# Three targets in turn for the last accumulated blocks of a mixture-of-experts stage

## The chip, the cores and the metric

The kernel runs on one core of a Trainium2 chip. The metric is the device time of one execution in microseconds (us). Four runs of the kernel before the change are given with their median; one more execution was recorded by the hardware profiler, and its trace gives all durations used here.

## The reference

The input `x` has 8 batches of 512 tokens with 256 numbers each, so 4096 tokens. Four layers follow each other, each of the form `x = x + layer(layernorm(x))`: a linear recurrence with projections, a mixture of experts, causal attention with 16 heads, and the same mixture of experts once more. Only the mixture matters for the change:

```python
topk_idx, tw = _route(x, router_w, bias)        # 4 of 16 experts for each token
combine = (one_hot(topk_idx, E) * tw[..., None]).sum(1)
h = einsum('td,edf->etf', x, gate_w);  u = einsum('td,edf->etf', x, up_w)
y = einsum('etf,efd->etd', silu(h) * u, down_w)
routed = einsum('etd,te->td', y, combine)       # sum of a token's 4 experts
sh = silu(x @ sh_gate_w) * (x @ sh_up_w) @ sh_down_w
return routed + sh                              # the layer adds x to this
```

So each of the 4096 output rows of the last layer is a sum of six terms: the row that went in, the shared experts' row, and four experts' rows with their weights.

## The kernel before

The kernel has four stages, one for each layer. In the two mixture stages (function `routed`, called with `i = 0` and, last, `i = 1`) the token rows have been sorted by expert into a DRAM tensor, and blocks of 128 rows of one expert are worked on one after the other. `LIKELY` = 136 blocks are run by `run(0, LIKELY)`; a rarely needed second run for blocks 136 to 142 stands in a branch before it. The blocks are ordered by batch: `DONE[b]` says from which block on no row of batch `b` can occur. The values are 31, 47, 63, 79, 95, 111, 127 for batches 0 to 6, then 135 for the first half of batch 7, and 143 for its second half.

For a block `n`, SP (SyncE) loads its rows (L982 to L990), ACT and DVE copy the two weight matrices (L1006), TensorE multiplies by them (L1033), ACT and DVE form the activation (L1041, L1043), and, two blocks later, `down(n)` multiplies by the third matrix (L1063), ACT scales the result by the routing weight (L1072), and POOL (GpSimd) issues an indirect DMA that adds the 128 result rows to rows of a DRAM tensor (L1073, destination `part`, source `rows`). In what follows this DMA is "the accumulation of block `n`".

Two accumulations on the same rows must not overlap. Therefore there are two DRAM tensors for each mixture, `parts[i][0]` and `parts[i][1]`, one with the stage's input in it and one with the shared experts' result, and blocks go to them in turn (`n % 2`). An accumulation waits until the one two blocks before it has landed; this wait stands in POOL's queue in front of the DMA, so that everything behind it on POOL waits too:

```python
if len(accs) > 1:
    behind_of(acc, accs[-2])
```

At the end the two parts are summed. For batches 0 to 6 of the last stage this is done in the middle of the run: some blocks after `DONE[b]`, `begin(b)` issues two loads of 512 KB on SP (L1609) that wait for the last two accumulations which can concern the batch (function `apart`), and later `add_up` adds them on DVE (L1613) and stores the sum in the output (L1614). The last batch is done in two halves of 256 rows behind block 135:

```python
plan.setdefault(LIKELY, []).append(begin_last)      # loads of the first half
routed(1, table, plan)
load_both(first + half, half, ends[1], (nc.sync, nc.scalar))
for n in range(2):
    add_up(first + n * half, half, ends[n])
```

`begin_last` declares the loads of the first half free of block 135's accumulation, and behind those of blocks 133 and 134. The loads of the second half wait for the last accumulation on the tensor that they read. The part 0 load of the second half is on SP's queue, the part 1 load on ACT's.

Small DMAs that prepare memory, among them the zeros for the spare rows of the parts (L351), are in a list `later`, of which each batch of the first stage issues a share behind its load of the next input (`Scan.load`, on SP's queue).

Of the kernel before, what the change touches and what calls it, by code (L numbers as in the profile page):

```python
# [10 lines left out]
FP = mybir.dt.float32  # L11
# [4 lines left out]
P = 128  # L16
SQ = 32
QUAD = P // SQ
B, T, D = 8, 512, 256
NT = T // P  # L20
# [14 lines left out]
NTOK = B * T  # L35
BLK = P
# [6 lines left out]
LIKELY = TK * NTOK // BLK + E // 2  # L43
# [9 lines left out]
DONE = [TK * rows // BLK + E - 1 for rows in KEYS]  # L53
# [29 lines left out]
def tile_hybrid_block(  # L83
# [22 lines left out]
    nc = tc.nc  # L106
# [8 lines left out]
    def bank(shape, name: str, kind: str = "one"):  # L115
        kind = instead.get(kind, kind)
        return stage[kind].tile(shape, FP, tag=kind, name=name)

    def banks_of(**many):
        pools = ExitStack()  # L120
        for kind, bufs in many.items():
            stage[kind] = pools.enter_context(
                tc.tile_pool(name=f"ps_{kind}", bufs=bufs, space=bass.MemoryType.PSUM)
            )
        return pools

    dram = ctx.enter_context(tc.tile_pool(name="dram", bufs=1, space=bass.MemoryType.DRAM))
# [2 lines left out]
    xg = [dram.tile([NROW, ROW], FP, name=f"xg_{i}") for i in range(2)]  # L130


    parts = [[dram.tile([NTOK + BLK, D], FP, name=f"part_{i}_{j}") for j in range(2)] for i in range(2)]

    x_tiles = {}

    def values(name: str):
        return work.tile([P, NT * (H * VC + 32 - VC)], FP, tag="v", name=name)
# [93 lines left out]
    def load_expert(e: int):  # L232
        at = e * WEXP
        gu = w_all[:, at : at + 2 * KD * F].rearrange("p (s k f) -> p s k f", k=KD, s=2)
        nc.sync.dma_start(out=gu[:, 0], in_=gate_w[e].rearrange("(p k) f -> p k f", p=P))
        nc.sync.dma_start(out=gu[:, 1], in_=up_w[e].rearrange("(p k) f -> p k f", p=P))
        nc.sync.dma_start(
            out=w_all[:, at + 2 * KD * F : at + WEXP].rearrange("p (k d) -> p k d", k=KF),
            in_=down_w[e].rearrange("(k p) d -> p k d", p=P),
        )  # L240
# [95 lines left out]
    zeros = const.tile([P, ROW], FP, name="zeros")  # L336
# [8 lines left out]
    later = [lambda e=e: load_expert(e) for e in range(E - OUT)]  # L345
    for i in range(2):
        later.append(
            lambda i=i: free(f"xg{i}", nc.sync.dma_start(out=xg[i][E * REG :, :], in_=zeros))
        )
        for j in range(2):  # L350
            later.append(lambda i=i, j=j: nc.sync.dma_start(out=parts[i][j][NTOK:, :], in_=zeros[:, 0:D]))  # L351
    shares = B - 2


# [144 lines left out]
    def kb4(name: str):  # L499
        return work.tile([P, NT, D], FP, tag="kb4", name=name, bufs=KB)  # L500
# [109 lines left out]
    every = [small.tile([P, len(KEYS), E], FP, tag="every", name=f"every_{i}", bufs=1) for i in range(2)]  # L610
# [196 lines left out]
    accs = []  # L807

    def apart(load, done: int):


        for n, acc in enumerate(accs):
            if n >= done:
                tc.declare_no_dep(load.ins, acc.ins, reason="no row of these tokens in later blocks")
            elif n >= done - 2:
                behind_of(load, acc)
        tc.add_to_no_dep_group("sums", load.ins)

    def behind_of(made, other):
        tc.add_manual_dep(  # L820
            made.ins,
            other.ins.name,
            mybir.DependencyInfo(mybir.DependencyClass.Sync, mybir.DependencyReason.DATA),
            reason="accumulations on the same rows",
        )

    def free(group: str, made):

        tc.declare_no_dep(made.ins, group=group, reason="rows of their own")
        tc.add_to_no_dep_group(group, made.ins)  # L830
# [103 lines left out]
    def routed(i: int, table, beside):  # L934

        weight_at, row_at, expert, many = table
# [122 lines left out]
        def down(n: int):  # L1059
            w, _, rows, act, gain = held.pop(n)  # L1060
            py = bank([P, D], f"pyr_{i}_{n}", "y")
            for f in range(KF):
                nc.tensor.matmul(  # L1063
                    py,
                    lhsT=act[:, f * P : (f + 1) * P],
                    rhs=w_all[:, bass.ds(w + 2 * KD * F + f * D, D)],
                    start=(f == 0),
                    stop=(f == KF - 1),
                )

            y = rows[:, ROW : ROW + D]
            nc.scalar.mul(y, py, gain[:, TK : TK + 1])  # L1072
            acc = nc.gpsimd.indirect_dma_start(  # L1073
                out=parts[i][n % 2],
                out_offset=bass.IndirectOffsetOnAxis(
                    ap=rows[:, D + 2 * TK : D + 2 * TK + 1].bitcast(U32), axis=0
                ),
                in_=y,
                in_offset=None,
                compute_op=ALU.add,  # L1080
            )
            if len(accs) > 1:
                behind_of(acc, accs[-2])
            tc.declare_no_dep(acc.ins, group="sums", reason="no row of those tokens in later blocks")
            accs.append(acc)

        def run(first: int, last: int):
# [18 lines left out]
            for n in range(first, last + 2):  # L1106
                load_to(n + AHEAD)
                if n + 2 < last and n + 2 not in known:
                    values(n + 2)
                if n + 1 < last:  # L1110
                    fetch(n + 1)
                if n + 2 not in heads and n + 2 < last:
                    turn(n + 2)
                if n < last:
                    up(n)
                if n + 1 in heads and n + 1 < last:
                    turn(n + 1)
                if n - 2 >= first:
                    down(n - 2)
                    for work_beside in beside.get(n - 1, ()):  # L1120
                        work_beside()
# [3 lines left out]
            many, min_val=0, max_val=NBLK, skip_runtime_bounds_check_because="a count of blocks"  # L1125
# [74 lines left out]
    class Attention:  # L1200
# [6 lines left out]
        bursts, parts = {}, {}  # L1207
# [167 lines left out]
    def prepared(b: int):  # L1375
# [17 lines left out]
        def begin():  # L1393
            held["added"] = load_sum(0, b, free_home("v", f"more_{b}"), lambda load: apart(load, first))
# [16 lines left out]


        plan = [begin, add, lambda: step(NT), lambda: step(1), lambda: step(NT + 1)]
        after = {}
        for at, do in zip((4, 12, 13, 14, 15), plan):
# [186 lines left out]
    with banks_of(big0=2, big1=2, misc=2, y=2):  # L1602

        def rows_at(of, first: int, many: int):
            return of[first : first + many, :].rearrange("(p t) d -> p t d", p=P)

        def load_both(first: int, many: int, both, queues=(nc.sync, nc.sync)):
            return [
                queue.dma_start(out=both[j], in_=rows_at(parts[1][j], first, many)) for j, queue in enumerate(queues)  # L1609
            ]  # L1610

        def add_up(first: int, many: int, both):
            tc.keep_in_program_order(nc.vector.tensor_add(both[0], both[0], both[1]))  # L1613
            nc.sync.dma_start(out=rows_at(out.rearrange("b t d -> (b t) d"), first, many), in_=both[0])  # L1614

        def homes(b: int):
            other = values(f"sum_{b}_1")[:, 0 : NT * D].rearrange("p (t d) -> p t d", t=NT)
            return xpool.tile([P, NT, D], FP, tag="x", name=f"sum_{b}_0"), other

        sums, plan = {}, {}  # L1620

        def begin(b: int):
            sums[b] = homes(b)
            for load in load_both(b * T, T, sums[b]):
                apart(load, DONE[b])

        for b in range(B - 1):
            wait, stay = (4, 12) if b < B - 2 else (1, 5)
            plan.setdefault(DONE[b] + wait, []).append(lambda b=b: begin(b))
            plan.setdefault(DONE[b] + stay, []).append(lambda b=b: add_up(b * T, T, sums[b]))  # L1630


        first, half, ends = (B - 1) * T, T // 2, []

        def begin_last():
            both = homes(B - 1)
            ends.extend([tile[:, n * NT // 2 : (n + 1) * NT // 2, :] for tile in both] for n in range(2))
            for load in load_both(first, half, ends[0]):
                apart(load, DONE[B - 1])

        plan.setdefault(LIKELY, []).append(begin_last)
        routed(1, table, plan)
        load_both(first + half, half, ends[1], (nc.sync, nc.scalar))
        for n in range(2):
            add_up(first + n * half, half, ends[n])

# [41 lines left out]
```

## Time and profile before

| what | value |
|---|---|
| runs | 1638.76, 1637.65, 1644.29, 1636.44 us |
| median of the four runs | 1638.21 us |
| profiled execution, own time | 1639.39 us |
| profiled execution, span of its instructions | 1637.7 us |
| mean granted TensorE clock | 0.985 |
| SP issues, loads of sums (L1609) | 17 on SP, 1 on ACT |
| SP issues, zeros of the parts (L351) | 4, 327 to 507 ns each, at 22.0 to 146.2 us |
| accumulations (L1073) | 272, 1542 to 2293 ns on POOL, median 1550 |
| additions of sums (L1613) | 7 of 128x1024 (about 1.21 us), 2 of 128x512 (0.69 us) |

The profile gives times in microseconds from the first instruction. PE is TensorE, PEld its weight loads, DVE VectorE, ACT ScalarE, POOL GpSimd, and SP SyncE; `SPq` and `ACTq` are DMA issues on these engines' queues. A row of the timeline has start, duration, engine, line, operation, tiles, and in brackets how long the engine was idle before and what seems to have ended that. The last stage's 136 blocks begin at about 1241 us. The releaser in brackets is inferred, and a wait for several things is put down to the one that came last.

### The profile page before, as it was taken

The numbers are of one execution on the slowest core, as the hardware profiler recorded it, in microseconds if no ns is written. First come the engines' busy times: TensorE is split into PE (matmuls) and PEld (weight loads), VectorE is DVE, ScalarE is ACT, GpSimd is POOL, SyncE is SP. The second block draws the span as 40 slices with busy tenths as digits, with TensorE's granted clock in tenths as the row PEclk, the third lists the DMA queues.
The fourth block names the chain that finished last, engine by engine and source line by source line (L and its number), as shares of the span: only waits on it lengthen the run. The fifth ranks groups of instructions, "written<-read, shape, count | busy, mean of one in ns | idle before, by whom it ended". The sixth has DMA issues, their size and how long they took to land. (4 is left out here: it accounts for less than half of the span.)

```text
span 1637.7 us, 34092 instructions
## 1 busy us (share of the span) xinstructions
PE 1580.4 (97%) x10030; PEld 1161.2 (71%) x10030; DVE 1004.5 (61%) x3264; ACT 779.5 (48%) x1622; POOL 775.0 (47%) x639
## 2 busy tenths in 40 slices
PE   8899998999999999999899999999999999999995
PEld 6466665679999999983444454444558999999995
DVE  6877764434466444437898889887834445444552
ACT  3343442235555555546544544454214555555553
POOL 4366754635556555540013432433432555555554
PEclk9999998999999999999999999999999999999998
DMA  5454423547777776641323433343745767777776
GB/s 169 137 178 154 149 99 125 180 92 109 117 122 108 107 98 96 93 68 46 80 83 114 121 109 108 106 118 98 261 138 90 109 112 127 119 138 131 136 136 128
DMA packets 282766, 196.88 MB, mean 120 GB/s; under 512 B 168689, under 2 KB 262673, under 8 KB 282577
## 3 DMA queue, kind: packets, MB, share of 16 engines
q1 hardware_dynamic: 230016, 121.50, 29.2%
q0 software_dynamic: 51984, 72.09, 24.8%
q8 instruction: 85, 1.39, 0.4%
q10 hardware_dynamic: 576, 1.05, 0.2%
q14 instruction: 105, 0.85, 0.2%
HBM read 91.29 MB, written 103.23 MB: 119 GB/s over the span
## 5 line engine op out<-in xcount | busy, mean ns | idle before, releaser
L1073 POOL DMA_INDIRECT part<-rows x272 | 426.8, 1569 | 342.9 <-ACT rows L1072 224.0
L798 POOL DMA_INDIRECT xg<-sorted_m,slots_m x256 | 270.4, 1056 | 260.6 <-ACT slots_m L795 128.8
L1033 PEld LDWEIGHTS ph<-rows,gate 128*128 128x128 f32 x2160 | 277.5, 191 | 32.7 <-ACT rows L1016 21.6
L1033 PE MATMUL ph<-rows,gate 128*128 128x128 f32 x2160 | 291.7, 278 | 0.5 <-ACT rows L1016 0.5
L1033 PE MATMUL ph<-rows,up 128*128 128x128 f32 x2160 | 285.3, 275 | 0.0
L1063 PE MATMUL pyr<-w_all,rows 128*128 x1088 | 279.5, 380 | 1.4 <-DVE rows L1043 1.4
L1033 PEld LDWEIGHTS ph<-rows,up 128*128 128x128 f32 x2160 | 262.9, 192 | 0.0
L1006 DVE COPY up<-w_all 128x512 f32 x270 | 120.0, 445 | 226.1 <-PE ph L1033 205.3
L1006 ACT COPY gate<-w_all 128x512 f32 x270 | 166.4, 617 | 124.3 <-DVE up L1006 60.1
L1043 DVE TENSOR_TENSOR rows<-ph,rows 128x256 f32<-128x256 f32 x272 | 115.5, 425 | 155.0 <-ACT rows L1041 75.3
L1295 ACT ACTIVATE w_all<-ps_a 128x1024 f32<-128x1024 f32 x160 | 155.2, 1021 | 105.4 <-PE ps_a L1285 93.3
L1063 PEld LDWEIGHTS pyr<-w_all,rows 128*128 128x128 f32 x1088 | 186.8, 192 | 15.8 <-DVE rows L1043 1.6
L1072 ACT ACTIVATE rows<-pyr,gain 128x256 f32<-128x256 f32 x272 | 128.7, 473 | 78.5 <-PE pyr L1063 58.0
L1041 ACT ACTIVATE rows<-ph 128x256 f32<-128x256 f32 x272 | 104.3, 384 | 117.2 <-PE ph L1033 101.1
L1174 PE MATMUL pd_m<-sd_sb,act_m 128*128 128x256 f32 x512 | 120.2, 383 | 6.2 <-DVE act_m L1162 3.4
L1285 PE MATMUL ps_a<-w_all 32*128 32x384 f32 (+3 forms) x1024 | 107.4, 474 | 10.9 <-ACT w_all L1295 9.7
L1174 PEld LDWEIGHTS pd_m<-sd_sb,act_m 128*128 128x128 f32 x512 | 95.9, 190 | 31.1 <-issue 9.4
L1305 DVE SCALAR_TENSOR_TENSOR w_all<-w_all,causal 128x512 f32<-128x512 f32 (+1 forms) x160 | 91.8, 574 | 28.2 <-ACT w_all L1295 26.2
L1285 PEld LDWEIGHTS ps_a<-w_all 32*128 32x128 f32 x1024 | 46.2, 187 | 68.6 <-ACT w_all L1295 36.0
L1146 PE MATMUL pg_m<-w_all,su_sb 128*128 128x512 f32 x192 | 93.2, 609 | 0.0
L1146 PE MATMUL pg_m<-w_all,sg_sb 128*128 128x512 f32 x192 | 92.8, 605 | 0.0
L1321 PE MATMUL po_a<-w_all,v_a 128*32 128x512 f32 (+3 forms) x1024 | 92.0, 450 | 0.0
(222 smaller groups left out, 1924.1 us busy)
## 6 DMA issues: line engine op xcount, KB each, us to landing
rows<-xg SPq DMA_DIRECT2D x720, 32.0 KB
rows<-xg SPq DMA_DIRECT2D x92, 134.0 KB
part<-x SPq DMA_DIRECT2D x16, 512.0 KB
w_all<-in_L_ffn_gate_w_dram SPq DMA_DIRECT2D x29, 256.0 KB
w_all<-in_L_ffn_up_w_dram SPq DMA_DIRECT2D x29, 256.0 KB
w_all<-in_L_ffn_down_w_dram SPq DMA_DIRECT2D x29, 256.0 KB
part<-ys_m SPq DMA_DIRECT2D x14, 512.0 KB
sum<-part SPq DMA_DIRECT2D x14, 512.0 KB
```

The costliest lines, as they stand in the source:

```text
L798: nc.gpsimd.indirect_dma_start(out=xg[i], out_offset=bass.IndirectOffsetOnAxis(ap=slots[:, at : at + 1], axis=0), in_=rows[:, t, :], in_of ...
L1006: copy(here, w_all[:, bass.ds(held[n][0] + half * KD * F, KD * F)])
L1033: nc.tensor.matmul(ph[s][:, f * P : (f + 1) * P], lhsT=both[s][:, k * F + f * P : k * F + (f + 1) * P], rhs=rows[:, ROW + k * P : ROW + (k ...
L1041: nc.scalar.activation(act, ph[0], AF.Silu)
L1043: made = nc.vector.tensor_mul(act, ph[1], act)
L1063: nc.tensor.matmul(py, lhsT=act[:, f * P : (f + 1) * P], rhs=w_all[:, bass.ds(w + 2 * KD * F + f * D, D)], start=(f == 0), stop=(f == KF - 1),
L1072: nc.scalar.mul(y, py, gain[:, TK : TK + 1])
L1073: acc = nc.gpsimd.indirect_dma_start(out=parts[i][n % 2], out_offset=bass.IndirectOffsetOnAxis(ap=rows[:, D + 2 * TK : D + 2 * TK + 1].bit ...
L1146: made = nc.tensor.matmul(dst, lhsT=w[:, k, f * P : (f + 1) * P], rhs=xnT[:, k, :], start=(k == 0), stop=(k == KD - 1),)
L1174: nc.tensor.matmul(py[:, j, :], lhsT=acts[n][:, f, t * P : (t + 1) * P], rhs=shared[n][3][:, f, :], start=(n == 0 and f == 0), stop=(n == ...
L1285: nc.tensor.matmul(ps[j // 2][:, j % 2, col : col + n], lhsT=k_sb[w][r, o, c * P : (c + 1) * P], rhs=q_sb[r, o, c * P : T], start=True, st ...
L1295: nc.scalar.activation(es[two], ps[two], AF.Exp, scale=ATT_SCALE)
```

## The change

A third DRAM tensor is made for the last mixture, `parts[1][2]`. Its rows 3584 to 4223 (the last batch and the spare rows) are filled with zeros by five DMAs of 128 KB in the list `later`. For blocks 128 to 135 of the last stage the target is `n % 3` instead of `n % 2`, and the accumulation waits for the one three blocks before it. The last batch's sum is made of three parts, with a third load for each half and one more addition for each half. The loads of all sums are issued in reversed order of their parts, and they wait for one more accumulation (three instead of two before `DONE`).

```diff
-    parts = [[... for j in range(2)] for i in range(2)]
+    parts = [[... for j in range(2 + i)] for i in range(2)]
...
+    for at in range(NTOK - T, NTOK + 1, P):
+        later.append(lambda at=at: nc.sync.dma_start(out=parts[1][2][at : at + P, :], in_=zeros[:, 0:D]))
...
-            elif n >= done - 2:
+            elif n >= done - 3:
                 behind_of(load, acc)
...
+            many = 3 if i == 1 and DONE[B - 2] < n < LIKELY else 2
             acc = nc.gpsimd.indirect_dma_start(
-                out=parts[i][n % 2],
+                out=parts[i][n % many],
...
-            if len(accs) > 1:
-                behind_of(acc, accs[-2])
+            if len(accs) >= many:
+                behind_of(acc, accs[-many])
...
-        def load_both(first: int, many: int, both, queues=(nc.sync, nc.sync)):
+        def load_all(first: int, many: int, homes, queues=(nc.sync, nc.sync, nc.scalar)):
             return [
-                queue.dma_start(out=both[j], in_=rows_at(parts[1][j], first, many)) for j, queue in enumerate(queues)
+                queue.dma_start(out=homes[j], in_=rows_at(parts[1][j], first, many))
+                for j, queue in reversed([*enumerate(queues[: len(homes)])])
             ]
 
         def add_up(first: int, many: int, both):
+            if len(both) > 2:
+                tc.keep_in_program_order(nc.vector.tensor_add(both[1], both[1], both[2]))
             tc.keep_in_program_order(nc.vector.tensor_add(both[0], both[0], both[1]))
...
         def begin_last():
-            both = homes(B - 1)
+            every = [*homes(B - 1), kb4(f"sum_{B - 1}_2")]
...
-            for load in load_both(first, half, ends[0]):
+            for load in load_all(first, half, ends[0], (nc.sync, nc.sync, nc.sync)):
                 apart(load, DONE[B - 1])
...
-        load_both(first + half, half, ends[1], (nc.sync, nc.scalar))
+        load_all(first + half, half, ends[1])
```

In the built programs the order of instructions on TensorE is the same before and after. DVE gains the two additions, SP the five zero writes and three more loads (the second half's part 1 load moves from ACT to SP, in front of the first half's loads), and ACT's one load is the second half of part 2 instead of part 1. On POOL only the targets and the waits of the last eight accumulations differ.

More of the change, by code (lines that the diff above doesn't have):

```diff
@@ L130, in tile_hybrid_block @@
     xg = [dram.tile([NROW, ROW], FP, name=f"xg_{i}") for i in range(2)]
-    parts = [[dram.tile([NTOK + BLK, D], FP, name=f"part_{i}_{j}") for j in range(2)] for i in range(2)]
+    parts = [[dram.tile([NTOK + BLK, D], FP, name=f"part_{i}_{j}") for j in range(2 + i)] for i in range(2)]
     x_tiles = {}
@@ L1623, in begin @@
             sums[b] = homes(b)
-            for load in load_both(b * T, T, sums[b]):
+            for load in load_all(b * T, T, sums[b]):
                 apart(load, DONE[b])
@@ L1635, in begin_last @@
         def begin_last():
-            both = homes(B - 1)
-            ends.extend([tile[:, n * NT // 2 : (n + 1) * NT // 2, :] for tile in both] for n in range(2))
-            for load in load_both(first, half, ends[0]):
+            every = [*homes(B - 1), kb4(f"sum_{B - 1}_2")]
+            ends.extend([tile[:, n * NT // 2 : (n + 1) * NT // 2, :] for tile in every] for n in range(2))
+            for load in load_all(first, half, ends[0], (nc.sync, nc.sync, nc.sync)):
                 apart(load, DONE[B - 1])
```

## The prediction

> **What bounds the kernel now.** I read the page first, then the last microseconds by stage, then the chain of waits there, and then POOL's timeline. TensorE carries nearly the whole span:
>
> ```profile
> PE 1580.4 (97%) x10030; PEld 1161.2 (71%) x10030; DVE 1004.5 (61%) x3264; ACT 779.5 (48%) x1622; POOL 775.0 (47%) x639
> ```
>
> The change touches no matmul, so it can win only where TensorE is idle at the end. The table of stretches (columns: stretch, length, busy time of PE, PEld, DVE, ACT, POOL with instruction counts, clock, DMA share, GB/s) shows that place:
>
> ```profile
> 1612.00:1618.00 6.00, 6.00 (x48) 5.79 (x47) 2.57 (x7) 2.47 (x6) 4.68 (x3) 1.00 0.55 119
> 1618.00:1621.00 3.00, 2.99 (x16) 2.27 (x14) 0.71 (x3) 0.95 (x2) 1.71 (x2) 1.00 0.56 68
> 1621.00:1630.00 9.00, 0.00 (x0) 0.00 (x0) 0.00 (x0) 0.47 (x1) 4.99 (x4) 0.73 0.59 67
> 1630.00:1637.70 7.70, 0.00 (x0) 0.00 (x0) 1.39 (x2) 0.00 (x0) 0.00 (x0) 0.50 0.53 195
> ```
>
> TensorE ends at 1621.0, and 16.7 us of the span follow it: 9 us of accumulations, then loads, an addition and a store. The chain of waits (start, length, what) says what they hang on:
>
> ```profile
> 1608.43 1.78 PE ph L1033 x16
> ...
> 1612.40 12.87 DMA part<-rows x5
> ...
> 1626.15 3.84 DMA part<-rows
> 1629.99 0.02 issue
> 1630.01 3.65 DMA sum<-part
> 1633.67 0.02 issue
> 1633.69 0.69 DVE sum L1613
> ```
>
> From 1612.40 on the chain is made of landings of accumulations. ACT's rows show when the last three results were ready, POOL's when blocks 128 to 135 were issued:
>
> ```profile
> 1619.30 0.47 ACT L1072 ACTIVATE rows<-pyr,gain 128x256 f32<-128x256 f32 x1 [1.38 <-PE pyr L1063]
> 1620.16 0.47 ACT L1072 ACTIVATE rows<-pyr,gain 128x256 f32<-128x256 f32 x1 [0.39 <-PE pyr L1063]
> 1621.07 0.47 ACT L1072 ACTIVATE rows<-pyr,gain 128x256 f32<-128x256 f32 x1 [0.44 <-ACT rows L1072]
> 1606.81 1.55 POOL L1073 DMA_INDIRECT part<-rows  x1 [0.30 <-issue]
> 1612.40 1.56 POOL L1073 DMA_INDIRECT part<-rows  x1 [4.04 <-ACT rows L1041]
> 1614.27 2.02 POOL L1073 DMA_INDIRECT part<-rows  x1 [0.30 <-ACT rows L1072]
> 1616.90 1.56 POOL L1073 DMA_INDIRECT part<-rows  x1 [0.61 <-issue]
> 1619.76 1.55 POOL L1073 DMA_INDIRECT part<-rows  x1 [1.29 <-issue]
> 1621.61 1.56 POOL L1073 DMA_INDIRECT part<-rows  x1 [0.30 <-ACT rows L1072]
> 1624.30 1.55 POOL L1073 DMA_INDIRECT part<-rows  x1 [1.12 <-issue]
> 1626.15 1.56 POOL L1073 DMA_INDIRECT part<-rows  x1 [0.30 <-issue]
> ```
>
> Block 135's result was ready at 1621.54 and was issued at 1626.15: 4.61 us lost. By the semaphore updates in the trace, the accumulations of blocks 127 to 135 landed at 1611.71, 1612.34, 1616.2, 1619.07, 1620.7, 1623.6, 1625.3, 1628.1 and 1629.99. So an accumulation takes about 3.8 us from its start (4.8 for block 130, and 6.77 for block 127, beside the two 512 KB loads of batch 6 issued at 1605.64), and the one two blocks later starts 0.69 us behind that landing. Two chains with a period of some 4.5 us give 2.25 us for a block, while POOL alone could issue each 1.86 us (1.55 busy and 0.30 between).
>
> **The change part by part.** *The wait for three blocks back.* I replay the eight issues: a start is the latest of ready, landing of three blocks back plus 0.69, and the previous start plus 1.86.
> - 128 starts at 1606.81 as before.
> - 129: ready at 1608.98, block 126 landed by 1605.6. Starts at 1609.0, was 1612.40.
> - 130: behind block 127's landing (1611.71): 1612.40.
> - 131: ready 1614.23, 1612.40 + 1.86: 1614.27. It takes the place and the 4.8 us of the old block 130: lands at 1619.07.
> - 132: ready 1617.17: 1617.2, lands at 1621.0.
> - 133: ready 1619.77: 1619.8, lands at 1623.7.
> - 134: 1619.8 + 1.86 = 1621.66, lands at 1625.5.
> - 135: 1621.66 + 1.86 = 1623.52; block 132's landing + 0.69 is 1621.7. Lands at 1623.52 + 3.84 = 1627.36.
>
> The last landing is 2.63 us earlier. What is late next is POOL's own pace, no longer the landing.
>
> *The loads.* Before, four loads of 256 KB were issued between 1628.15 and 1630.01 and landed at 1631.76, 1632.44, 1633.07 and 1633.67: 3.61 us for the first, then 0.63 apart. After, there are six. The part 1 load of the second half stands first on SP and goes at block 133's landing, 1623.7. Four more (three on SP 0.43 apart, one on ACT) go at block 134's landing, 1625.5, and land, by these rows, at 1629.1, 1629.75, 1630.4 and 1631.0. The last, part 0 of the second half, goes at 1627.36: it lands at 1631.0 if it only has its own 3.65 us, at 1631.65 if it stands in line. That is 2.0 to 2.65 us earlier than 1633.67.
>
> *The two additions*, 0.69 us each. For the first half both end by about 1631.15; the second half's first addition needs ACT's load of part 2 (1631.0), and runs to 1631.84, the last to 1632.53. Before, it ended at 1634.38: a gain of 1.85. If the part 2 load comes last in the line (1631.65), both additions lie on the path, and it is 1633.07, a gain of 1.3. If the last load has its 3.65 us and part 2 is early, it is 1631.7, a gain of 2.65. I take 1.8, near the middle case, as the line of landings is what the four loads before showed. The store and the end behind it (1634.38 to 1637.7) stay.
>
> [...]
>
> *The zeros.* Five DMAs on SP in the first stage; the same issue at L351 took 0.33 to 0.51 us, so at most 2.5 us of SP's queue, in front of loads of the next input and stores. The waits of SP show 191.4 us on these stores (L1444) for DVE, which hides them; I take 0. If that cover is gone it is 2.5. I see no way to a gain.
>
> *The third accumulation in `apart` and the reversed order of loads*: for batches 0 to 6 the third one is awaited by a later one anyhow, and both loads are needed by the one addition. The cost is a semaphore wait of 0.03 us (as those in front of L1609) on SP. I take 0.
>
> The sum: 1639.39 - 1.8 = 1637.6 us for an execution like the profiled one. The median of the four runs is 1.18 below that one, so the prediction goes from the median: 1638.21 - 1.8 = 1636.4 us.
>
> **The rivals.** *A, the forecast*: 1.3 to 2.65 us gained, 1636.4. For it speaks that the gap from ready to issue (4.61 us) lies on the chain.
>
> *B, the gain goes to the line of loads.* 512 KB more go through the same transfers. The two 512 KB loads of batch 6, beside accumulations, landed at 1609.28 and 1611.26, that is 5.6 us for 1 MB, or 1.0 us for each further 256 KB in place of 0.63. Five loads from 1625.5 then end at 1625.5 + 3.65 + 4 x 1.0 = 1633.15; with two additions 1634.5, against 1634.38. No gain: 1638.2. Against it: the four loads at the end, without accumulations beside them, had 0.63.
>
> *C, slower: loads go ahead of the last accumulation.* Now one load is issued at block 133's landing and four more in one burst at block 134's, while block 135 is under way. Were its accumulation held up as that of block 127, it would land at 1623.52 + 6.77 = 1630.29, the last load at 1633.94, and with one or two additions the end is 1634.63 to 1635.32, or 0.25 to 0.95 later than now: 1638.5 to 1639.2, I take 1638.8. It decides from where block 135 needs more than 6.47 us. Against it: before, loads were issued 2.0 us behind block 135's start too, and it landed in 3.84.
>
> *D, the wait isn't what spaces POOL*: then nothing moves, and the addition on the path makes it 1638.9. The idle 1.29 and 1.12 us with results ready speak against it.
>
> **How the numbers follow.** A 0.62, B 0.18, C 0.13, D 0.07. A measurement of this kernel can tell about 0.3% from no change, 4.9 us, and no case by itself reaches it: TensorE's own end stays. Beyond it lie only runs that scatter (1.77 us below the median to 6.08 above). Faster by over 0.3% needs 3.1 us more than A: 0.10. Slower by over 0.3% needs C with the zeros unhidden and scatter: 0.05. Within: 0.85. The range: A's best, 1638.21 - 2.65, with the scatter below of 1.77 is 1633.8; C's worst, 1639.16, with 0.55 (the second highest run over the median) is 1639.7.
>
> **What would show it.** In the profile after: POOL's eight issues at the starts above, the last near 1623.5 with a busy row each 1.86 us; the last `sum<-part` issued near 1627.4 and taking 3.65 in the chain; four small additions at L1613's place; TensorE's end unchanged at 1621.0. B would show the last load over 5 us behind its issue; C a last accumulation over 6 us; D the old spacing. The prediction is wrong if TensorE's end moves by more than 2 us, since then something in front of the tail was touched.

## The result and the profile after

The changed kernel took **1641.98 us** (median of 52 runs, 1636.79 to 1648.93) beside 1638.42 us for the kernel before (78 runs on the same chip). The ratio is 1.0021 with a 95% interval of 1.0013 to 1.0029, so it is about 3.5 us slower (2.1 to 4.8). That is inside the 0.3% that got the chance 0.85, but it has the other sign than the forecast, and 1641.98 is 2.3 us above the upper end of the range. The profiled execution took 1644.22 us itself, with a span of 1642.5.

TensorE's work is what it was, as the page's first line says:

```profile
PE 1580.8 (96%) x10030; PEld 1162.4 (71%) x10030; DVE 1005.3 (61%) x3266; ACT 779.1 (47%) x1622; POOL 774.3 (47%) x639
```

The table of stretches (stretch, length, busy time of PE, PEld, DVE, ACT, POOL, clock, DMA share, GB/s), cut at the places that answer to the four rows of before:

```profile
1616.50:1622.50 6.00, 6.00 (x48) 5.79 (x48) 2.57 (x7) 2.47 (x6) 3.75 (x3) 1.00 0.64 133
1622.50:1625.50 3.00, 2.99 (x16) 2.28 (x14) 0.71 (x3) 0.95 (x2) 1.95 (x2) 1.00 0.56 68
1625.50:1634.50 9.00, 0.00 (x0) 0.00 (x0) 0.00 (x0) 0.47 (x1) 3.73 (x3) 0.63 0.76 155
1634.50:1642.50 8.00, 0.00 (x0) 0.00 (x0) 2.68 (x4) 0.00 (x0) 0.00 (x0) 0.50 0.37 139
```

Two things are to be seen. TensorE ends at 1625.5 in place of 1621.0, that is 4.5 us later, though none of its instructions changed. And 17.0 us of the span still follow it, with four additions on DVE where there were two: the tail that was to become shorter did not.

POOL's timeline (start, duration, operation, tiles, idle time before and its releaser) for blocks 128 to 135, with ACT's row of block 135's result:

```profile
1610.83 1.55 POOL L1076 DMA_INDIRECT part<-rows  x1 [1.04 <-ACT rows L1074]
1613.77 1.56 POOL L1076 DMA_INDIRECT part<-rows  x1 [1.38 <-DMA part<-rows]
1616.37 1.55 POOL L1076 DMA_INDIRECT part<-rows  x1 [1.04 <-ACT rows L1074]
1619.02 1.79 POOL L1076 DMA_INDIRECT part<-rows  x1 [1.10 <-ACT rows L1074]
1621.95 1.55 POOL L1076 DMA_INDIRECT part<-rows  x1 [1.15 <-ACT rows L1074]
1624.55 1.56 POOL L1076 DMA_INDIRECT part<-rows  x1 [1.05 <-ACT rows L1074]
1626.42 1.55 POOL L1076 DMA_INDIRECT part<-rows  x1 [0.31 <-ACT rows L1074]
1628.27 1.56 POOL L1076 DMA_INDIRECT part<-rows  x1 [0.30 <-issue]
1625.58 0.47 ACT L1074 ACTIVATE rows<-pyr,gain 128x256 f32<-128x256 f32 x1 [0.44 <-PE pyr L1065]
```

This is as forecast: the last three blocks follow at POOL's own pace of 1.86 us, and block 135 is issued 2.22 us after its result (1626.05), not 4.61. The chain of waits behind it (start, length, what):

```profile
1628.27 4.38 DMA part<-rows
1632.65 0.02 issue
1632.67 4.59 DMA sum<-part
1637.27 0.03 issue
...
1637.35 0.69 DVE sum L1618
1638.05 0.02 issue
1638.07 0.69 DVE sum L1619
```

The last load takes 4.59 us in place of 3.65, and two additions follow it in place of one. The chain puts both behind that load because it landed last before them, but the load is that of part 0, which only the last addition reads, and it had landed 0.8 us before that one began. What the end waited for is shown by DVE's timeline, where all four additions stand in one row:

```profile
1636.01 0.69 DVE L1618 TENSOR_TENSOR sum<-sum,sum 128x512 f32<-128x512 f32 x1 [12.28 <-DMA sum<-part]
1636.74 0.69 DVE L1619 TENSOR_TENSOR sum<-sum,sum 128x512 f32<-128x512 f32 x1
1637.35 0.68 DVE L1618 TENSOR_TENSOR sum<-sum,sum 128x512 f32<-128x512 f32 x1
1638.07 0.69 DVE L1619 TENSOR_TENSOR sum<-sum,sum 128x512 f32<-128x512 f32 x1
```

The sums of the parts begin only at 1636.01, 10.9 us after TensorE's last matmul began, and then need 2.75 us. So the third part's price ate what the earlier accumulation won. The two profiled spans differ by 4.8 us, and 4.5 of them arise far ahead of the changed code. Followed instruction by instruction, TensorE is 0.5 us ahead of before up to 1136 us, and 4.5 us behind from 1218 us on. There, at the end of attention and in the last routing, the same table of stretches shows for before, and then for after:

```profile
1176.00:1180.00 4.00, 3.47 (x23) 1.80 (x24) 3.33 (x13) 1.85 (x9) 2.55 (x3) 1.00 0.21 68
1210.00:1214.00 4.00, 3.46 (x16) 3.07 (x17) 3.61 (x16) 0.77 (x3) 0.04 (x1) 1.00 0.55 178
1214.00:1218.00 4.00, 4.00 (x17) 2.76 (x16) 0.00 (x0) 0.68 (x2) 2.46 (x3) 1.00 0.19 69
```

```profile
1176.00:1180.00 4.00, 3.00 (x19) 1.31 (x20) 3.31 (x8) 1.14 (x7) 2.50 (x3) 0.65 0.20 63
1210.00:1214.00 4.00, 2.02 (x5) 1.66 (x6) 2.66 (x13) 0.00 (x0) 1.05 (x2) 0.67 0.62 201
1214.00:1218.00 4.00, 4.00 (x11) 3.19 (x10) 1.16 (x4) 0.77 (x3) 0.40 (x1) 0.50 0.13 40
```

The column before the last two is the granted clock: TensorE ran at half of it in two short stretches that before does not have, for 3.41 us from 1177.23 us and for 6.83 us from 1211.36 us.

### The profile page after: what moved, and what is told of

Same layout as the page of the kernel before. It is cut to its first block, busy times and chain, and to the rows that moved or that the text cites. A ratio compares the mean times of both kernels' runs of the same rounds, so it can differ in the third digit from the quotient of the medians.

```text
span 1642.5 us, 34115 instructions
## 1 busy us (share of the span) xinstructions
PE 1580.8 (96%) x10030; PEld 1162.4 (71%) x10030; DVE 1005.3 (61%) x3266; ACT 779.1 (47%) x1622; POOL 774.3 (47%) x639
```

## The experiments

Three theories. **T**: the change costs time in the last stretch, since the sum in three parts (six loads, four additions) costs more than the earlier accumulations win. **U**: something is lost upstream as well, by the zeros, by the third tensor, or by half-clock stretches that the change brings. **L**: the profile that the forecast stood on is usual in its last stretch, so that three targets do win about 2 us there. "Last stretch" is from the start of TensorE's last matmul to the span's end; the place of an instruction is counted from the same start.

The chips differ: the kernel before runs at 1638.4 us on the first one and at 1639.1 on that of e9 to e12, but at 1616.9 to 1617.9 on the other three, so each ratio is to before on its own chip. The results together:

| run | kernel | ratio to before | 95% interval | last stretch, us |
|---|---|---|---|---|
| first | after | 1.0021 | 1.0013 to 1.0029 | 17.40 |
| e1 | after | 1.0002 | 0.9993 to 1.0011 | 16.84 |
| e8 | after | 1.0007 | 0.9997 to 1.0016 | 17.03 |
| e9 | after | 1.0023 | 1.0008 to 1.0037 | 17.38 |
| e14, e16 | after, one profile each | - | - | 17.36, 17.97 |
| first | before | 1 | - | 17.05 |
| e5, e12, e15 | before, one profile each | - | - | 15.27, 15.25, 15.36 |
| e2 | zeros and third tensor alone | 0.9994 | 0.9985 to 1.0003 | 15.21 |
| e10 | the same | 0.9997 | 0.9981 to 1.0014 | 15.89 |
| e4 | after, zeros written later | 1.0007 | 0.9998 to 1.0016 | 18.20 |
| e3 | three-part sum, two targets | 0.9994 | 0.9985 to 1.0003 | 16.39 |
| e6 | three targets, two-part sum | 0.9993 | 0.9983 to 1.0003 | 15.17 |
| e13 | the same | 0.9994 | 0.9984 to 1.0004 | 15.21 |
| e7 | block 135 alone to a third target | 0.9992 | 0.9981 to 1.0003 | 14.69 |
| e11 | the same | 0.9999 | 0.9985 to 1.0013 | 15.07 |

**Is the loss there again? (e1, e8, e9)** The changed kernel as it is.

> The changed kernel once more, on the chip and beside the runs that the next three are compared with. The result on record is 3.5 us slower than before (interval 2.1 to 4.8). Theory T (the tail): the three-part sum costs more than the earlier accumulations win, so the time from TensorE's last matmul to the end is longer than before's 16.7 us in most executions. Theory U (upstream): something that the five zero writes or the third tensor change in front of the last stage, above all stretches at half the TensorE clock, costs the 3.5 us, and the tail is even. Both expect 2 to 5 us slower here.

> The changed kernel a third time, beside the two runs above. Theory T: a tail 1 to 2 us longer than that of before, so 1 to 2 us slower (0.06 to 0.12%), whatever the chip. Theory U: between no loss (as in the second comparison, +0.3 us) and the 3.5 us on record, by how the half-clock stretches fall, with a tail as long as before's.

> The changed kernel once more, timed against before. T (the tail alone): its last stretch, from the start of TensorE's last matmul to the span's end, is 16.8 to 17.5 us against 15.2 to 15.3 for before, so +1.5 to +2.2 us, a ratio of 1.0009 to 1.0014 wherever it runs. U (something is lost upstream as well): +3.5 us, 1.0021, with TensorE's last matmul itself starting some 1.5 us or more later than before's.

On the two chips that run before at about 1617 us it loses 0.3 us (-1.1 to 1.8) and 1.1 us (-0.5 to 2.6), neither distinguishable from none, and on the other 3.8 us (1.3 to 6.1). The 2 to 5 us that both theories expected of e1 were missed. The last stretch is 16.84, 17.03 and 17.38 us. The chain of e9, the last one, has the same steps as the first profile of after, within 0.25 us:

```profile
1627.03 4.17 DMA part<-rows
1631.20 0.02 issue
1631.21 4.73 DMA sum<-part
...
1636.08 0.70 DVE sum L1618
1636.78 0.02 issue
1636.80 0.69 DVE sum L1619
```

**How usual was the first profile of before? (e5, e12, e15)** The kernel before, unchanged.

> The kernel before once more, for its tail. Its first profile had block 135 issued 4.61 us after its result and a tail of 17.05 us from the start of TensorE's last matmul to the end; the run with zeros only, which has the same tail by construction, had 2.83 us and 15.21 us. Theory T (the gain was overrated since the first profile caught a late tail, and the three-part sum costs about what it showed) expects a tail near 15.2 us here, with block 135 issued about 2.8 us after its result. Theory L (the first profile's tail is the usual one) expects 17 us and 4.6 us.

> Before itself, for one more profile of its last stretch. T: block 135 is issued 2.8 to 2.9 us after its result and the last stretch is 15.2 to 15.3 us, as in its second profile, or up to 4.6 and 17.05 us as in its first, if an accumulation of batch 6's or 7's early blocks is late by 2 us. A second profile near 15.2 makes the first one the exception; one near 17 makes it usual and the forecast's base right.

> Before, one more profile. T: last stretch 15.2 to 15.3 us again, or up to 17.05; half-clock stretches near 1177 and 1211 us can occur in before too. U: none of them in before, as in its first and third profile.

The last stretch was 15.27, 15.25 and 15.36 us, so the 17.05 us of the first profile were the exception. Before's chain and POOL's last three issues in e12:

```profile
1625.77 4.82 DMA part<-rows
1630.59 0.02 issue
1630.61 2.60 DMA sum<-part
1633.20 0.02 issue
1633.23 0.69 DVE sum L1613
```

```profile
1621.38 1.56 POOL L1073 DMA_INDIRECT part<-rows  x1 [1.05 <-ACT rows L1072]
1623.25 1.55 POOL L1073 DMA_INDIRECT part<-rows  x1 [0.30 <-ACT rows L1072]
1625.77 1.56 POOL L1073 DMA_INDIRECT part<-rows  x1 [0.97 <-issue]
```

Block 135 is issued 2.89 us behind its result; these three have 2.87 to 2.93, and the other three profiles with two targets (e2, e3, e10) 2.83 to 3.02. Only the first profile has 4.61. Its delay came in with block 129, which stood 3.41 us behind its result as it waited for block 127's accumulation of 6.77 us; in the six others it stood 0.80 to 2.07 us behind, and the distance was worked off by block 133 (0.27 or 0.28 us; 1.84 in the first). So L falls: three targets win 0.6 to 0.8 us of issue, not 2.6. And of the last two blocks only 135 gains by it: block 134, whose landing releases the loads of the first half, is issued 1.28 us behind its result in after's first profile and in five of these six (1.49 in e2), so those loads start no sooner than usual.

**The zeros and the third tensor (e2, e10, e4).** In e2 and e10 the kernel before gets the tensor and its writes, which nothing uses:

```diff
+        parts[1] has three tensors
+    for at in range(NTOK - T, NTOK + 1, P):
+        later.append(lambda at=at: nc.sync.dma_start(out=parts[1][2][at : at + P, :], in_=zeros[:, 0:D]))
```

> Only the third tensor and the five zero writes in the first stage; the last eight accumulations, the loads and the additions are those of before. Theory T expects no difference (within 1 us). Theory U expects the whole loss, 2 to 5 us slower.

> Before with the third target and its writes of zeros, which nothing uses. T: same as before within 0.8 us (0.9995 to 1.0005), last stretch 15.2 to 17.1 us as before's. U through the zeros or the third target: +1.5 us or more, 1.0009 or above, arising before the last stretch.

In e4 the changed kernel writes them in the last stage, behind blocks 40 to 48, in place of the first:

```diff
-        later.append(lambda at=at: nc.sync.dma_start(out=parts[1][2][...], in_=zeros[:, 0:D]))
+            plan.setdefault(40 + 2 * n, []).append(
+                lambda at=at: nc.sync.dma_start(out=parts[1][2][at : at + P, :], in_=zeros[:, 0:D])
+            )
```

> The changed kernel with the five zero writes moved from the first stage to the last one (blocks 40 to 48, where TensorE is never idle). Theory T expects the loss on record, 2 to 5 us slower. Theory U, as far as the zero writes cause it, expects no loss: within 1 us of before.

The zeros alone give 0.9994 and 0.9997, no loss, on a chip of either kind, though on the slower kind the interval leaves room for up to 2.3 us. Moving them wins nothing: 1.0007 (1.1 us, -0.3 to 2.6, which decides between neither forecast), beside 1.0002 for after on the same chip. So no cost of theirs was measured, as the forecast took it.

**The sum's three parts without the third target (e3), and the third target without the third part (e6, e13).** In e3 `many` is always 2, so that the third part stays zeros; in e6 and e13 blocks 128 to 135 go to three targets and the last batch's sum leaves the third one out (its output lacks that part).

```diff
-            many = 3 if i == 1 and DONE[B - 2] < n < LIKELY else 2
+            many = 2                                    # e3
...
-            every = [*homes(B - 1), kb4(f"sum_{B - 1}_2")]
+            every = homes(B - 1)                        # e6, e13
```

> The changed kernel, but blocks 128 to 135 go to two targets in turn as before; the third part holds only zeros and is still loaded and added. Theory T: the whole price of the three-part sum shows without the earlier accumulations (2.4 us in the profile after, by block 135's issue against its result), so 4 to 7 us slower. Theory U: about the loss on record plus whatever the tail now costs, also 3.5 to 7 us; what tells them apart is the tail in the trace and the run with zeros only.

> The changed kernel with three targets, but the third part is neither loaded nor added, so the last batch's rows lack what blocks 128, 131 and 134 gave. Theory T: the tail loses the price of the three-part sum and keeps the earlier accumulations: about 14.6 us from the start of TensorE's last matmul (15.2 less 0.6 earlier issue), so 0.5 to 1 us faster than before and 1.5 to 2.5 us faster than the changed kernel. Theory U (the loss lies upstream of the tail) expects the whole time to stay at that of the changed kernel.

> After without the third part in the last sum (that part is left out of the output). Its program up to the last batch's sum is after's. T (the last stretch alone; the rest is scatter): last stretch 15.1 to 15.3 us as before's, same as before within 0.8 us, ratio 0.9995 to 1.0005, and the stretch from 1136 to 1216 us as long as before's within 3 us either way. U (after's program loses upstream too): +1.5 us or more, 1.0009 or above, and the stretch from 1136 to 1216 us 3 to 5 us longer than before's, as in after's two profiles.

With the third part's loads and additions alone, the last stretch is 16.39 us, 1.1 above before's usual. Its time, 0.9994 (-2.4 to 0.5 us), shows no loss and has no room for 1.1 us, let alone for the 4 to 7 that T expected and the 3.5 to 7 of U; here the price stands in one profile and not in the times. Nor does e3 bring the six loads together: the second half's part 2 load, with no late accumulation to wait for, was issued 21 us before TensorE's last matmul, and the sums began 9.31 us behind that matmul's start, as in before. The 1.1 us are one more addition in front of the end (some 0.65 us) and a longer end (some 0.45 us). With the third target alone the last stretch is 15.17 and 15.21 us (T expected 14.6 of e6). The chain of e13:

```profile
1604.42 4.97 DMA part<-rows
1609.39 0.02 issue
1609.41 2.85 DMA sum<-part
...
1612.35 0.69 DVE sum L1619
```

Without the third part the last load takes 2.85 us (3.32 in e6), against 4.46 to 5.04 in the six profiles of after, and one addition follows it. The sums begin at 9.49 us (9.54 in e6), counted from the start of TensorE's last matmul, against 10.34 to 11.48 in after and 9.29 to 9.52 in before's three later profiles. The last load is issued 0.4 to 1.1 us earlier than in those three, but only 0.2 or 0.3 us of it are left at the last addition's end. Against after on the same chip, e6 has 0.9993 to e8's 1.0007: leaving out the third part wins some 2.3 us, near the 1.9 us between their last stretches (the means of the twelve runs of each lie 2.1 us apart). T is shown in the last stretch. It is the third part that costs, and the third target by itself wins almost nothing.

**A smaller dose (e7, e11).** Only block 135 goes to a third target, so only the last half of the sum has a third part, and the loads of the other parts keep their order:

```diff
+            alone = i == 1 and n == LIKELY - 1
-                out=parts[i][n % 2],
+                out=parts[i][2 if alone else n % 2],
-            if len(accs) > 1:
+            if len(accs) > 1 and not alone:
                 behind_of(acc, accs[-2])
```

> Only block 135 goes to the third target and waits for no accumulation; blocks 128 to 134 go to two targets as before; three zero writes, and only the last half of the last batch has a third load and a second addition. Theory T: block 135 is issued 2.2 us after its result as with three targets, at the price of one load and one addition that lies ahead of the last load: 0 to 0.6 us faster than before, and 1 to 2 us faster than the changed kernel. Theory U: as slow as the changed kernel.

> Only block 135 goes to a third target, which only the sum's last half loads and adds. T: last stretch 14.5 to 15.0 us, 0.5 to 0.7 us below before's usual 15.2, so 0.9995 to 0.9997 (and 0.9986 if before's last stretch here is the 17.05 us of its first profile). U: +0.5 to +1 us, as the zeros cost upstream what the last stretch wins.

The last stretch is 14.69 and 15.07 us, the shortest two of all (T's 14.5 to 15.0 for e11 was just missed), and the ratios are 0.9992 and 0.9999, neither distinguishable from 1. DVE's timeline of e7 shows how little is left to win this way: there are still three additions in a row.

```profile
1609.71 0.69 DVE L1619 TENSOR_TENSOR sum<-sum,sum 128x512 f32<-128x512 f32 x1 [10.71 <-DMA sum<-part]
1610.34 0.69 DVE L1618 TENSOR_TENSOR sum<-sum,sum 128x512 f32<-128x512 f32 x1
1611.07 0.69 DVE L1619 TENSOR_TENSOR sum<-sum,sum 128x512 f32<-128x512 f32 x1
```

These sums begin 9.34 us behind the start of TensorE's last matmul (9.50 in e11), against 10.34 to 11.48 in after. As in after, one load goes ahead and the first half's follow block 134's landing; but three loads stand in that burst, where after has a fourth, ACT's.

**Is the upstream loss the change's? (e14, e16, and the stretch in all profiles)**

> After, one more profile. T: from 1136 to 1216 us of the program TensorE is as far behind before's as the executions of before are among themselves (about 1 to 3 us), last stretch 16.8 to 18.2 us. U: 3 to 5 us behind before's there again on a chip that runs before at 1638, with half-clock stretches near 1177 and 1211 us.

> After, one more profile. T: as in the run before last, with other half-clock stretches. U: the same two half-clock stretches as in its first and fourth profile, near 1177 and 1211 us, 3 to 5 us behind before's.

These two fell on a chip of 1617.87 us for before, so they say nothing of the slower ones. The table gives TensorE's time from one fixed instruction of it at 1136 us to another at 1220 us of the first profile of before, 337 weight loads later:

| chips that run before at | before | after | zeros alone | block 135 alone |
|---|---|---|---|---|
| 1638 to 1639 us | 83.34, 83.17 | 88.33, 87.00 | 83.60 | 82.73 |
| 1617 to 1618 us | 73.29, 73.27 | 71.72, 73.30, 73.24, 73.24 | 73.25 | 73.31 |

On the quicker chips nothing is lost there (the other four profiles on them, of e3, e4, e6 and e13, have 73.2 to 73.3). On the slower ones both profiles of after lose 3.7 to 5.2 us, and the four of other kernels do not, though TensorE's instructions are the same and in the same order. What is seen in it: TensorE waits at the down matmuls of the routing stage near 1211 us for 2.90 us in before, 2.14 in e12, 2.92 and 2.85 in after, 1.00 in the zeros alone and 1.0 with block 135 alone, and no such wait stands out on a quicker chip. Behind it the clock is halved for 6.83 and 3.41 us in the two profiles of after, and in none of the other four. The wait of equal length in before was not followed by it. In the first profiles of before and after the starts of the half clocks lie whole multiples of 3.41 us apart (34.13 us from 1177.23 to 1211.36 in after, ten times that). Counted in such steps from a half clock's start, the step in front of the half clock near 1211 us has TensorE busy for 1.12 us in after and 0.56 in e9, while the wait of before lies across two steps with 2.34 and 1.59 us of work, that of e12 across two with 3.01 and 1.67. But before has half clocks right behind steps with 2.50 and 2.68 us of work too (from 741.09 and 1137.04 us): that it matters where a wait falls was the author's guess, and is not shown. (An earlier half-clock stretch, of 3.41 us near 1177 to 1182 us, stands in both profiles of after, with the zeros alone and with block 135 alone, and in neither of before. These four have zero writes in common, but the stretch in the table is no longer with the zeros alone and with block 135 alone, so this half clock is not what is lost.) Two profiles against four cannot tell a cause from scatter, and no instruction of the change runs near that place. **This part stays open.**

## Why the prediction was wrong

The working of the last stretch, from the start of TensorE's last matmul, in two profiles of each kernel:

| step, us | before, first | before, e12 | after, first | after, e9 |
|---|---|---|---|---|
| last accumulation has landed | 9.38 | 8.64 | 7.54 | 7.33 |
| its load, from issue (+0.02) | 3.65 | 2.60 | 4.59 | 4.73 |
| from there to the last addition's end | 0.72 | 0.72 | 1.50 | 1.55 |
| store and the end | 3.27 | 3.27 | 3.75 | 3.75 |
| sum | 17.05 | 15.25 | 17.40 | 17.38 |

In before the end waits for the load of the second row. In after it doesn't: the additions of the first half begin late and the other two stand in their row, so that the last load is in 0.8 us before it is read.

- **The wait for three blocks back** went as replayed: spacing 1.86 us, block 135 issued 2.22 us behind its result (forecast 1.98). What failed is its base: "4.61 us lost" was read from one execution, and is 2.83 to 3.02 in the six other profiles with two targets. From the usual base the step wins 0.6 to 0.8 us of issue. The prediction itself noted block 127's 6.77 us as out of line, and yet kept the distance that followed from it. The accumulation of block 135 took 4.38 and 4.17 us, not 3.84 (4.75 to 4.82 in before's later profiles). And after's end no longer hangs on block 135: the first half's loads are released by block 134, which goes 1.28 us behind its result with three targets and, usually, with two.
- **The loads** are the mis-sized term. The forecast gave 3.6 us for the first of the burst and 0.63 for each next. In after's first profile the four loads issued behind block 134's landing (5.12 to 6.13 in the count above) landed at 10.04, 10.22, 10.81 and 11.49, where the forecast had 8.5 to 10.4: the first took 4.9 us. In e12 three loads, issued at 5.11 to 5.95, landed at 8.81, 9.36 and 9.99. So the first half's sums began at 10.90 in after and at 9.45 in e12, though the loads went at the same time. This later start, with a fourth load in the burst, is what the end waited for. The last load, forecast at 3.65 to 4.3 us, took 4.59, and 4.46 to 5.04 in the other profiles of after, but was in 0.8 to 0.9 us before it was read. (SP issues 19 loads of sums in after and 17 in before, two more and not three.)
- **The additions**: forecast one or two after the last load, with the first half's out of the way by then. The first half's loads came so late that all four stood in a row, and the last ended at 13.65 us in the count above, against 11.9 in the forecast (1632.53 less 1620.61) and 13.78 in before's first profile. The forecast gain of 1.85 us was 0.13 there, and against e12's 11.98 it is a loss of 1.7.
- **The store and the end**, taken as unchanged, are 0.48 us longer. They are 3.27 to 3.34 in the profiles of before and 3.75 to 3.79 in those of after and in e3 (4.49 in e4), but 3.72 and 3.74 with the zeros alone as well, and 3.30 to 3.44 in e6, e7, e11 and e13. The difference lies between the last store's issue and its landing (2.45 us in after's first profile, 2.03 in e12). What makes it was not tried.
- **The zeros** at 0, and the third wait in `apart` at 0: right, by e2, e10 and e6.
- **The rivals.** B named the right mechanism: the line of loads took the gain. Its split of it was another, 3.65 us for the first load and 1.0 for each next where 4.9 and 0.2 to 0.7 were measured, and its sign, a last load over 5 us, shows in one of six profiles of after (5.04). Its end of the last addition at 1634.5, 13.9 in the count above, is near the measured 13.65, which is in part luck. Its time of 1638.2 holds no loss against the median, because it too stood on the first profile's tail. C fell: block 135's accumulation stayed under its 6.47 us. D fell: POOL did move up.
- **The range** ended at C's 1639.16 plus scatter. It lacked a case with B's line on a usual tail, which gives 17.3 (the mean of the six profiles of after) less 15.3 (of the three later ones of before) = +2.0 us, or 1640.2. That much the runs show: on average the sums begin 1.4 us later, 0.2 us more go from there to the last addition's end, and 0.45 us more to the store and the end. The first comparison's 3.5 us has 2.1 as its lower bound, and on the quicker chips 2.0 lies within e8's interval and just above e1's (1.8). The rest on the slower chips, some 1.5 us, is the open part above.
- The sign by which the prediction was to be seen wrong, TensorE's end moving by over 2 us, was too narrow: TensorE's last matmul begins at 1620.6 and 1621.95 us in two profiles of before, and at 1624.0 with the zeros alone.

Before's last load in e12, issued 2.7 us behind the three others, took 2.60 us; the last load of after, with four others not yet landed, took 4.46 to 5.04. The two added loads, with the additions behind them, cost the 2.0 us above; no run here moves the same bytes in fewer transfers.

## What to carry to other kernels

Before a wait in the tail becomes a term of a sum, it should be read in several executions, and a distance that begins at one odd transfer is not to be trusted (here 4.61 us, usually 2.9). When a chain of updates is split over more targets, ask which landing releases the first loads of the reduction and whether the change moves that one (here block 134's, which it did not), count the loads at the price that they have in company, and see whether its additions still fit in front of the last landing. The smallest dose is worth a run: here one block to a third target had the shortest tails, and even those could not be told from no change in time.

## What the runs showed of the hardware

- Until TensorE's last matmul, each stretch at half the granted clock lasted 3.41 us or a small multiple (3.41, 6.83, 10.24). One begins between 804 and 821 us in all 18 profiles, and one between 1138 and 1145 us in all but one; others, as those near 1177 and 1211 us, stand only in some. No run shows what sets them off: a wait of 2.9 us near 1211 us was followed by a half clock in after's first profile and not in before's.
- From POOL's start to its landing, block 135's accumulation of 128 rows took 3.84 to 4.82 us in the four profiles of before, and 3.84 to 5.80 over all profiles.
- Loads of 256 KB in a burst, from the first issue to the first landing: 2.85 to 3.82 us with three loads within 0.9 us (nine profiles), 4.33 to 5.60 with four within 1.1 us, of which one on ACT (the six of after and e4).
- The kernel before ran at 1638.4 and 1639.1 us on two chips and at 1616.9 to 1617.9 us on three, with some 10 of the 20 us in the routing between 1136 and 1220 us (83.3 against 73.3 us).
